# Another order for the products of layer 0 beside an eigensolver: turned rows in place, W3 in halves, G·s1 by batch

## Chip, cores and metric

One core of one Trainium2 chip. The metric is the device time of one launch in microseconds (us). Everything is float32.

## What is computed

Two residual layers with a norm ahead of each, on x (64 batches, 256 nodes, 256 features) and one adjacency matrix `adj` (256 x 256):

```python
h = relu(layernorm(x))                       # layer 0
G = adj * adj
s1 = relu(G @ (h  @ W1))                     # W1: 256 x 512
s2 = relu(G @ (s1 @ W2))                     # W2: 512 x 1024
x  = x + G @ (s2 @ W3)                       # W3: 1024 x 256
h = relu(layernorm(x))                       # layer 1
L = D^-1/2 (diag(deg) - adj) D^-1/2          # only the lower triangle counts
_, U = eigh(L)
x  = x + U @ (relu((U.T @ h) @ W1' + b1) @ W2' + b2)
```

The products of layer 0 may be bracketed in any way, and so may `(U.T @ h) @ W1'`.

## The kernel before

Two bodies of work share the core until layer 1 begins. `Eigen.vectors` finds U: 254 Householder steps (lines 252 to 331), then 32 QL steps on small blocks (lines 563 to 700), then four levels that join the blocks (lines 1024 to 1436). It is one long chain of mostly small VectorE (DVE) operations. ScalarE (ACT) takes square roots and squares in it, and TensorE (PE) turns columns into rows: the matmuls into `psA` and `psB` at line 252 come once in each Householder step. `Layers.layer0` is independent of it and consists of large products.

Layer 0 works on 32 pairs of batches. Each stage of a pair is a method of `Layers`; all products are issued by `group` (line 1527), so the trace tells them apart by tile names. A float32 matmul shows as two records.

- `begin(q)`: loads x (a tag with 2 buffers), `norm` (four ACT sums, a DVE operation, four ACT squares, then an ACT root among seven DVE operations, lines 1529 to 1551), `relu_norm` into `h0`.
- `first(q)`: y1 = turned G·h0, 16 records `bank<-gt,h` with 256 columns, four banks, copied out by ACT (line 1572).
- `second(q)`: y1·W1, 16 records `bank<-L_gnn_W,y` with 512 columns, one bank for each half m of the rows and batch b; ACT makes s1 of each bank with a relu (line 1615). Then y2 = turned G·s1, 32 records `bank<-gt,s` with 256 columns, four banks through `project`, each with both batches of one block c.
- `third(q)`: W2·y2, 64 records `bank<-y,L_gnn_W` with 512 columns, eight banks, relu into s2 (line 1625).
- `fourth(q)`: s2·W3, 64 records `bank<-L_gnn_W,s` with 256 columns, two banks (one for each half m of the rows), copied to p3 (line 1639).
- `last(q)`: G·p3, 8 records `bank<-p,gt` with 512 columns, two banks, which DVE adds to x to give x1 (line 1648); x1 goes to DRAM for all but the last two pairs; then `norm` and `relu_norm` into h1.
- `for_layer1(q)`: turns h1 by 8 transposes (`bank<-eye,h`, line 1666) in two banks, ACT copies each to `ht` (line 1669), then 16 records `bank<-L_gnn_W,ht` with 128 columns make hw (copied at line 1682, sent to DRAM).

What sets the order: each engine has one list of instructions, fixed when the program is built. A planner of the language simulates the program and gives an engine that is free the earliest instruction in the program's text that is ready. All of `eigen.vectors` is written ahead of `layer0`, so the eigensolver goes first wherever it is ready and layer 0 fills what is left, in the order of its own text. [...] The result shows in the trace: PE's list has one to ten records of layer 0 between two of the eigensolver, and in every pair the same order, `first(q+1)`, `last(q)`, `second(q+1)`, `third(q+1)`, the transposes of `for_layer1(q)`, then 2 records of hw, 2 or 4 of W3, 14 of hw, and the rest of W3.

All work tiles of layer 0 have one buffer; `ht` shares the tag and so the buffer of `p3`. Four PSUM banks (tag `bank`) go round among all stages of layer 0; the eigensolver has the other four. Layer 1 (`layer1`, lines 1754 to 1770) has its order written out by hand and begins after both; `eigen.mend`, a branch that isn't taken here, stands before it.

Of the kernel before, what the change touches and what calls it, by code (L numbers as in the profile page):

```python
# [21 lines left out]
F32 = mybir.dt.float32  # L22
# [5 lines left out]
N = 256  # L28
P = 128
H = 2  # L30
PAIRS = 32
# [1440 lines left out]
class Layers:  # L1472
# [102 lines left out]
    def layer0(self):  # L1575


        self.begin(0)
        self.first(0)
        self.second(0)  # L1580
        for q in range(PAIRS):
            if q + 1 < PAIRS:
                self.begin(q + 1)
            self.third(q)
            if q > 0:
                self.for_layer1(q - 1)
            self.fourth(q)
            if q + 1 < PAIRS:
                self.first(q + 1)
            self.last(q)  # L1590
            if q + 1 < PAIRS:
                self.second(q + 1)
        self.for_layer1(PAIRS - 1)

    def begin(self, q):
# [10 lines left out]
    def second(self, q):  # L1606

        nc, w1, y1 = self.nc, self.w["L0_gnn_W1"], self.y1.pop(q)
        s1 = self.wp.tile([P, H, 2, 512], F32, tag="s1", name="s1")
        for m in range(H):  # L1610
            for b in range(2):
                ps = self.bank()
                at = b * N + m * P
                self.group(ps, [(y1[:, c, at : at + P], w1[:, c, :]) for c in range(2)])
                nc.scalar.activation(s1[:, m, b, :], ps, AF.Relu)  # L1615
        self.y2[q] = self.project(s1, 512 // P, self.gt2, "y2")

    def third(self, q):

# [4 lines left out]
            self.group(ps, [(w2[:, c, j * P : (j + 1) * P], y2[:, c, :]) for c in range(4)])  # L1624
            nc.scalar.activation(s2[:, j, :], ps, AF.Relu)  # L1625

    def fourth(self, q):

        nc, w3, s2 = self.nc, self.w["L0_gnn_W3"], self.s2.pop(q)
        self.p3[q] = p3 = self.wp.tile([P, H, 2 * N], F32, tag="p3", name="p3")  # L1630
        for m in range(H):
            ps = self.bank()
            for b in range(2):
                at = b * N + m * P
                self.group(
                    ps[:, b * N : (b + 1) * N],
                    [(s2[:, j, at : at + P], w3[:, j, :]) for j in range(1024 // P)],
                )
            nc.scalar.copy(p3[:, m, :], ps)

    def last(self, q):

# [11 lines left out]
        self.norm(x1, scale, shift)  # L1654
        self.h1[q] = self.relu_norm(x1, scale, shift, "h1")

    def for_layer1(self, q):

        nc, h1 = self.nc, self.h1.pop(q)
        ht = self.wp.tile([P, N // P, 2 * N], F32, tag="p3", name="ht")  # L1660
        for c in range(N // P):
            ps = self.bank()
            for b in range(2):
                for h in range(H):
                    at = b * N + h * P
                    nc.tensor.transpose(  # L1666
                        ps[:, at : at + P], h1[:, h, b, c * P : (c + 1) * P], self.eye
                    )
            nc.scalar.copy(ht[:, c, :], ps)  # L1669
        hw = self.kept.tile([P, H, 2, P], F32, tag="hw", name="hw")  # L1670
        ps = self.bank()
        for h in range(H):
            for b in range(2):
                at = (h * 2 + b) * P
                self.group(
                    ps[:, at : at + P],
                    [
                        (ht[:, c, b * N + h * P : b * N + (h + 1) * P], self.w["L1_gnn_W1"][:, c, :])
                        for c in range(N // P)
                    ],  # L1680
                )
        nc.scalar.copy(hw.rearrange("p h b k -> p (h b k)"), ps)  # L1682
        if q in self.spilled:
            nc.sync.dma_start(out=self.spilled_hw[q], in_=hw.rearrange("p h b k -> p (h b k)"))
        else:
            self.hw[q] = hw
# [142 lines left out]
```

## Time and profile before

| | us |
|---|---|
| median of 3 runs | 2566.05 (2566.05 to 2566.56) |
| the profiled execution | 2568.63, of which its span is 2566.5 |
| the eigensolver's Householder steps end | about 1400 |
| its QL steps | 1437 to 1805 |
| its last DVE work | about 2250 |
| the last product of layer 0 ends | 2395.6 |
| layer 1 | 2396 to 2566 |

The profile has a row of busy time for each engine, tables of busy time by stretch of time, lists of who waited for whom, and a timeline of each engine. "PE" is matmuls, "PEld" the loads of the stationary operand. "bank<-gt,s" means: writes a tile `bank`, reads `gt` and `s`. In a timeline, "[3.22 <-ACT s L1615]" means that the engine was idle for 3.22 us just before and that ACT's instruction of line 1615, which writes tile s, ended that. Full-speed rows of a product start 0.429 us apart at 512 columns, 0.216 at 256 and 0.110 at 128 (medians over all pairs of neighbours of one kind).

### The profile page before, as it was taken

What the parts mean: (1) busy time and instruction counts of PE and PEld (TensorE: products, weight loads), DVE (VectorE), ACT (ScalarE), POOL (GpSimd) and SP (SyncE); (2) the same over time, 40 slices, a digit from 0 to 9 for tenths busy, and PEclk for the clock granted to TensorE, in tenths of its full rate; (3) what the DMA queues carried; (4) which work ended last, traced back from release to release, by engine and by line L of the source; (5) the groups of instructions that cost most, each with busy time, mean ns of one, the idle gap of its engine ahead of it and who ended that gap; (6) DMA issues with size and microseconds to landing.
All of it is one profiled execution on the core that took longest, in us unless ns stands there. A gap on an engine that the chain in (4) does not pass through costs nothing. (4 is left out here: it accounts for less than half of the span.)

```text
span 2566.5 us, 38939 instructions
## 1 busy us (share of the span) xinstructions
PE 2457.2 (96%) x8986; PEld 1524.1 (59%) x8986; DVE 2186.7 (85%) x13785; ACT 1025.5 (40%) x3080; POOL 473.7 (18%) x2006
## 2 busy tenths in 40 slices
PE   7999999999999999999999998899999999999899
PEld 4566566556665555555555555556556656666688
DVE  7999999999999999999999999999889899810343
ACT  4444344444443344444434433333444342343322
POOL 1222222222222233333332000000000000000343
PEclk9999999999999999999999999999999999999999
DMA  3000000000000000000000000000000000020376
GB/s 114 17 21 21 21 5 21 21 17 22 21 22 21 5 22 22 17 22 22 22 7 20 17 21 22 21 22 5 25 22 21 21 21 12 14 71 1 123 252 208
DMA packets 59405, 90.07 MB, mean 35 GB/s; under 512 B 5792, under 2 KB 42784, under 8 KB 59168
## 3 DMA queue, kind: packets, MB, share of 16 engines
q1 hardware_dynamic: 59168, 87.52, 10.3%
q8 instruction: 74, 1.21, 0.2%
q14 instruction: 163, 1.34, 0.2%
HBM read 47.13 MB, written 40.37 MB: 34 GB/s over the span
## 5 line engine op out<-in xcount | busy, mean ns | idle before, releaser
L1527 PE MATMUL bank<-y,L_gnn_W 128*128 128x512 f32 x2048 | 923.4, 593 | 0.0
L1527 PEld LDWEIGHTS bank<-y,L_gnn_W 128*128 128x128 f32 x2048 | 373.4, 192 | 369.6 <-issue 350.5
L1527 PE MATMUL bank<-L_gnn_W,s 128*128 128x256 f32 x2048 | 474.5, 380 | 0.0
L1527 PEld LDWEIGHTS bank<-L_gnn_W,s 128*128 128x128 f32 x2048 | 377.3, 192 | 44.6 <-ACT s L283 0.3
L1625 ACT ACTIVATE s<-bank 128x512 f32<-128x512 f32 x256 | 151.3, 592 | 297.7 <-PE bank L1527 296.9
L1527 PE MATMUL bank<-gt,s 128*128 128x256 f32 x1024 | 249.6, 392 | 18.6 <-ACT s L1615 18.3
L1527 PE MATMUL bank<-L_gnn_W,y 128*128 128x512 f32 x512 | 234.4, 594 | 4.9 <-DVE x L1648 3.2
L1527 PEld LDWEIGHTS bank<-gt,s 128*128 128x128 f32 x1024 | 195.2, 198 | 64.2 <-ACT s L1615 29.2
L1727 POOL TENSOR_TENSOR xb<-x,ub 128x512 f32<-128x512 f32 x64 | 79.8, 1269 | 650.3 <-DVE x L1648 558.1
L273 ACT ACTIVATE junk<-xr 128x254 f32<-128x254 f32 (+63 forms) x254 | 77.9, 307 | 300.8 <-DVE xr L131 298.7
L274 POOL COPY alpha<-xr 128x1 f32<-128x1 f32 x254 | 100.8, 397 | 497.0 <-DVE xr L131 478.5
L1527 PEld LDWEIGHTS bank<-L_gnn_W,y 128*128 128x128 f32 x512 | 92.7, 191 | 103.6 <-issue 80.1
L1557 ACT ACTIVATE h<-x,shift,scale 128x256 f32<-128x256 f32 x256 | 133.8, 589 | 40.0 <-DVE shift L1551 39.8
L1536 ACT ACTIVATE junk<-x 128x256 f32<-128x256 f32 x256 | 106.0, 414 | 87.9 <-DVE x L1648 73.8
L1572 ACT COPY y<-bank 128x512 f32<-128x512 f32 x192 | 109.9, 577 | 77.3 <-PE bank L1527 76.9
L131 DVE SCALAR_TENSOR_TENSOR A<-wr,uc,A 128x255 f32<-128x255 f32 (+63 forms) x381 | 139.7, 367 | 0.0
L1540 ACT ACTIVATE junk<-x,nm 128x256 f32<-128x256 f32 x256 | 129.2, 505 | 18.3 <-DVE nm L1537 12.2
L252 PEld LDWEIGHTS psA<-ident,A 128*128 128x128 f32 x381 | 51.0, 134 | 143.8 <-PE bank L1527 63.0
L327 POOL TENSOR_TENSOR e<-nb,alpha 128x1 f32<-128x1 f32 x254 | 48.2, 190 | 458.2 <-DVE nb L139 433.3
L131 DVE SCALAR_TENSOR_TENSOR q<-q 128x1 f32<-128x1 f32 (+1 forms) x576 | 121.1, 210 | 12.9
L131 DVE SCALAR_TENSOR_TENSOR A<-xr,wc,A 128x255 f32<-128x255 f32 (+63 forms) x381 | 128.7, 363 | 0.0
L252 PEld LDWEIGHTS psB<-ident,ac 128*128 128x128 f32 x381 | 44.0, 134 | 136.3 <-PE bank L1527 68.5
(623 smaller groups left out, 4611.7 us busy)
## 6 DMA issues: line engine op xcount, KB each, us to landing
x<-x SPq DMA_DIRECT2D x60, 512.0 KB, 3.6
x<-in_x_dram SPq DMA_DIRECT2D x64, 256.0 KB, 3.8
out_dram<-out SPq DMA_DIRECT2D x64, 256.0 KB, 2.2
hw<-hw SPq DMA_DIRECT2D x60, 256.0 KB, 2.7
L_gnn_W<-in_L_gnn_W_dram SPq DMA_DIRECT2D x1, 2048.0 KB, 10.9
L_gnn_W<-in_L_gnn_W_dram SPq DMA_DIRECT2D x1, 1024.0 KB, 13.4
L_gnn_W<-in_L_gnn_W_dram SPq DMA_DIRECT2D x1, 512.0 KB, 6.3
mask<-in_c_blk_dram SPq DMA_DIRECT2D x2, 256.0 KB, 2.8
```

Source lines behind the costliest of these rows:

```text
L131: return self.nc.vector.scalar_tensor_tensor(out, in0, scalar, in1, op0, op1, accum_out=accum)
L252: nc.tensor.transpose(ps[:, h * P : (h + 1) * P], column[:, h : h + 1].to_broadcast([P, P]), ident[:, 0, 0:P],)
L273: nc.scalar.activation(sq[:, rest], xr[:, rest], AF.Square, accum_out=tail)
L274: nc.gpsimd.tensor_copy(alpha, xr[:, lo : lo + 1])
L327: nc.gpsimd.tensor_tensor(e0, nb, alpha, OP.add)
L1527: self.nc.tensor.matmul(out, lhsT=lhsT, rhs=rhs, start=i == 0, stop=i == len(pairs) - 1)
L1536: nc.scalar.activation(junk, x[:, j // 2, j % 2, :], AF.Copy, accum_out=s[:, j : j + 1])
L1540: nc.scalar.activation(junk, x[:, j // 2, j % 2, :], AF.Square, bias=nm[:, j : j + 1], accum_out=v[:, j : j + 1])
L1557: self.nc.scalar.activation(h[at], x[at], AF.Relu, bias=shift[:, j : j + 1], scale=scale[:, j : j + 1])
L1572: self.nc.scalar.copy(out[:, c, :], ps)
L1625: nc.scalar.activation(s2[:, j, :], ps, AF.Relu)
L1727: nc.gpsimd.tensor_tensor(xb[:, :, b, :], x1[:, :, b, :], self.ub2, OP.add)
```

## The change

Each product keeps its records, sizes and count; so do the copies and the DVE work. What changes is the order of the program's text in a pair's turn of the loop:

| | before | after |
|---|---|---|
| 1 | begin(q+1) | begin(q+1) |
| 2 | third(q): W2 | third(q): W2 |
| 3 | transposes, copies and hw of q-1 | transposes and copies of q-1 (`turn_rows`) |
| 4 | W3, both halves | W3, half 0 |
| 5 | first(q+1) | hw of q-1 (`for_layer1`) |
| 6 | last(q) | first(q+1) |
| 7 | second(q+1) | W3, half 1 |
| 8 | | second(q+1) |
| 9 | | last(q) |

In `second`, the W1 banks of batch 0 come first, then those of batch 1; G·s1 is then done for batch 0 (two banks, each with two blocks c) and after that for batch 1. The copy to y2 writes two runs of 256 columns instead of one of 512. `turn_rows` takes two banks, transposes into both, and only then copies both back into the buffer of h1 itself, so that `ht` is no longer a tile and `p3` has its buffer alone.

```diff
         for q in range(PAIRS):
-            if q + 1 < PAIRS:
+            more = q + 1 < PAIRS
+            if more:
                 self.begin(q + 1)
             self.third(q)
             if q > 0:
+                self.turn_rows(q - 1)
+            self.fourth(q, 0)
+            if q > 0:
                 self.for_layer1(q - 1)
-            self.fourth(q)
-            if q + 1 < PAIRS:
+            if more:
                 self.first(q + 1)
+            self.fourth(q, 1)
+            if more:
+                self.second(q + 1)
             self.last(q)
-            if q + 1 < PAIRS:
-                self.second(q + 1)
+        self.turn_rows(PAIRS - 1)
         self.for_layer1(PAIRS - 1)
...
         s1 = self.wp.tile([P, H, 2, 512], F32, tag="s1", name="s1")
-        for m in range(H):
-            for b in range(2):
+        for b in range(2):
+            for m in range(H):
                 ps = self.bank()
                 at = b * N + m * P
                 self.group(ps, [(y1[:, c, at : at + P], w1[:, c, :]) for c in range(2)])
                 nc.scalar.activation(s1[:, m, b, :], ps, AF.Relu)
-        self.y2[q] = self.project(s1, 512 // P, self.gt2, "y2")
+        self.y2[q] = y2 = self.wp.tile([P, 512 // P, 2 * N], F32, tag="y2", name="y2")
+        for b in range(2):
+            for c in range(0, 512 // P, 2):
+                ps = self.bank()
+                for i in range(2):
+                    at = (c + i) * P
+                    self.group(
+                        ps[:, i * N : (i + 1) * N],
+                        [(s1[:, h, b, at : at + P], self.gt2[:, h, :]) for h in range(H)],
+                    )
+                nc.scalar.copy(
+                    y2[:, c : c + 2, b * N : (b + 1) * N], ps.rearrange("p (c n) -> p c n", c=2)
+                )
...
-    def fourth(self, q):
...
-        for m in range(H):
...
+    def fourth(self, q, m):
+
+        nc, w3, s2 = self.nc, self.w["L0_gnn_W3"], self.s2[q]
+        if q not in self.p3:
+            self.p3[q] = self.wp.tile([P, H, 2 * N], F32, tag="p3", name="p3")
+        ps = self.bank()
...
-    def for_layer1(self, q):
-
-        nc, h1 = self.nc, self.h1.pop(q)
-        ht = self.wp.tile([P, N // P, 2 * N], F32, tag="p3", name="ht")
-        for c in range(N // P):
-            ps = self.bank()
+    def turn_rows(self, q):
+
+        nc, h1 = self.nc, self.h1[q]
+        banks = [self.bank() for _ in range(N // P)]
+        for c, ps in enumerate(banks):
             for b in range(2):
                 for h in range(H):
                     at = b * N + h * P
                     nc.tensor.transpose(
                         ps[:, at : at + P], h1[:, h, b, c * P : (c + 1) * P], self.eye
                     )
-            nc.scalar.copy(ht[:, c, :], ps)
+        for c, ps in enumerate(banks):
+            nc.scalar.copy(h1[:, c].rearrange("p b f -> p (b f)"), ps)
+
+    def for_layer1(self, q):
+
+        nc, ht = self.nc, self.h1.pop(q).rearrange("p c b f -> p c (b f)")
```

More of the change, by code (lines that the diff above doesn't have):

```diff
@@ L1625, in third @@
             nc.scalar.activation(s2[:, j, :], ps, AF.Relu)
-    def fourth(self, q):
-        nc, w3, s2 = self.nc, self.w["L0_gnn_W3"], self.s2.pop(q)
-        self.p3[q] = p3 = self.wp.tile([P, H, 2 * N], F32, tag="p3", name="p3")
-        for m in range(H):
-            ps = self.bank()
[L1633 to L1639, printed above, removed]
+    def fourth(self, q, m):
[3 more added lines that the diff above has]
+        ps = self.bank()
+        for b in range(2):
+            at = b * N + m * P
+            self.group(
+                ps[:, b * N : (b + 1) * N],
+                [(s2[:, j, at : at + P], w3[:, j, :]) for j in range(1024 // P)],
+            )
+        nc.scalar.copy(self.p3[q][:, m, :], ps)
     def last(self, q):
@@ L1655, in last @@
         self.h1[q] = self.relu_norm(x1, scale, shift, "h1")
-    def for_layer1(self, q):
-        nc, h1 = self.nc, self.h1.pop(q)
-        ht = self.wp.tile([P, N // P, 2 * N], F32, tag="p3", name="ht")
-        for c in range(N // P):
-            ps = self.bank()
+    def turn_rows(self, q):
+        nc, h1 = self.nc, self.h1[q]
+        banks = [self.bank() for _ in range(N // P)]
+        for c, ps in enumerate(banks):
             for b in range(2):
```

## The prediction

> **What bounds the kernel now.** I read the page's busy row and slices first, then busy time by stretch, then who waited for whom, then timelines of PE and ACT at the waits that the change is about.
>
> ```profile
> PE 2457.2 (96%) x8986; PEld 1524.1 (59%) x8986; DVE 2186.7 (85%) x13785; ACT 1025.5 (40%) x3080; POOL 473.7 (18%) x2006
> PE   7999999999999999999999998899999999999899
> DVE  7999999999999999999999999999889899810343
> ```
>
> The first row of slices must be read against the second: PE is full from end to end, DVE is as full until the eigensolver ends at slice 35. Two full engines side by side: which one gives way decides the gain.
>
> ```profile
> 64.00:800.00 736.00, 727.61 (x2709) 432.97 (x2709) 717.63 (x4229) 321.71 (x998) 189.44 (x812) 1.00 0.06 19
> 800.00:1400.00 600.00, 582.27 (x2096) 332.26 (x2095) 576.15 (x4263) 265.01 (x917) 186.78 (x1051) 1.00 0.06 19
> 1400.00:1800.00 400.00, 370.60 (x1297) 233.38 (x1297) 370.82 (x2953) 143.51 (x405) 7.53 (x36) 0.98 0.05 17
> 1800.00:2255.00 455.00, 431.60 (x1525) 271.73 (x1524) 398.50 (x1960) 179.16 (x503) 0.48 (x2) 0.98 0.06 22
> 2255.00:2396.00 141.00, 129.52 (x451) 81.14 (x449) 11.84 (x37) 46.83 (x114) 9.87 (x8) 0.96 0.07 25
> ```
>
> The columns are the stretch, its length, and the busy time of PE, PEld, DVE, ACT and POOL. PE is idle 8, 18, 29, 23 and 11 us in these stretches; busy time flatters it, so I also took, from the starts of all PE records in the timeline, the time between neighbours over the full-speed distance (0.429, 0.216, 0.110 us). By the record that came late:
>
> | us lost before | 64-800 | 800-1400 | 1400-1800 | 1800-2255 | 2255-2396 |
> |---|---|---|---|---|---|
> | eigensolver's records | 26.6 | 40.2 | 1.8 | 11.7 | 0 |
> | hw | 3.7 | 3.7 | 13.7 | 12.4 | 3.4 |
> | G·s1 | 0.5 | 0.0 | 19.0 | 12.8 | 0.7 |
> | W1, last | 0.1 | 0.1 | 10.1 | 0.1 | 0.1 |
> | transposes | 0 | 0 | 0 | 1.6 | 11.0 |
>
> The change aims at hw, G·s1, W1 and last: 80 us, of which 2.5 (hw of the last pair) and the 11.0 of the last transposes lie behind the end of layer 0, where nothing can be put between. So 77.8 us can be reached, 68 of them between 1400 and 2255. What ends these waits:
>
> ```profile
> PE bank L1527 <- ACT ht L1669: 22.3, 27, 4.8
> PE bank L1527 <- ACT s L1615: 20.0, 15, 3.4
> ACT rts L608 <- DVE cs L139: 101.5, 25, 9.7
> DVE x L1648 <- PE bank L1527: 78.5, 6, 54.0
> ```
>
> Each row gives the sum, how many, the longest. PE waits for ACT, and the third row says why ACT is late: line 608 is the eigensolver's root in a QL step, and ACT stands before it until DVE delivers. The fourth is the opposite wait; 74 of its 78 us come after 2255 (in the timeline, 19.8 and 54.0), so while the eigensolver runs DVE practically never waits for layer 0.
>
> ```profile
> 1484.28 0.23 ACT L608 ACTIVATE rts<-cs 128x32 f32<-128x32 f32 x1 [6.11 <-DVE cs L139]
> 1485.52 0.22 ACT L630 ACTIVATE q<-q 128x15 f32<-128x15 f32 x1 [1.01 <-DVE q L131]
> 1485.64 0.57 ACT L1639 COPY p<-bank 128x512 f32<-128x512 f32 x1
> 1495.89 0.23 ACT L608 ACTIVATE rts<-cs 128x32 f32<-128x32 f32 x1 [9.69 <-DVE cs L139]
> 1496.03 0.57 ACT L1639 COPY p<-bank 128x512 f32<-128x512 f32 x1
> ```
>
> From one root to the next is 11.6 us, DVE's step, and ACT has been waiting for up to 9.7 of them. The second p copy stands behind the root though its bank was ready. Here layer 0 runs ahead and is held by its place in ACT's list. Of 31 roots' intervals, those with W2 alone carry three banks, 3 x 8 x 0.429 = 10.3 us of PE for 11.6 us of time: PE must be idle 1.3 us in each, wherever it waits.
>
> [...] the p copy just shown waits behind another instruction's wait. [...] the busy row shows 109 us of idle PE, distances between starts 202.
>
> **The change, part by part.** Records, copies, DVE operations and transfers keep their number and size, so only waits count. The moves pass no queue of POOL; the x1 store and the loads of the next x keep their order on SP and only shift with `last`.
>
> *Cover per pair.* hw gets W3's half 0 between it and the copies (32 x 0.216 = 6.9 us); last gets `second` (14 us) behind its second p3 copy in place of first (3.4); first's y1 copies get 6.9 in place of 3.4 us; G·s1 had 1.7 us for batch 0 and 0.9 for batch 1 after the last W1 bank, and gets 3.4 each. y2 now has `last` (3.4) ahead of W2. W3's half 0 loses hw ahead of it (2 us), but its first use of the last s2 block comes 3 us in; I price that at nothing. Cover exceeds nearly all waits of the rows above (longest 5.0). If time were PE's waits, 77.8 us would go.
>
> *What comes in their place.* From 800 to 2255 DVE is the limit (followed back from the eigensolver's end, the chain of work is 59 to 95% DVE in each 200 us there). PE's list is fixed, and DVE passes through it at its own pace: what PE saves at G·s1 it waits later, at the next ACT or eigensolver record. The gain is then not the wait removed but how much more of layer 0 the planner places beside a given piece of the eigensolver, since that is taken off the 140 us after 2255, where PE alone sets the pace.
>
> *How much more it places.* In the Householder steps this can be counted: the PE time of layer 0's records between two `psB` groups is what the planner thought fits. Over 248 steps it falls smoothly (6.1 us early to 3.3 late, scatter 0.26). Fitted with DVE's layer-0 operations allowed for, a step with W1 to G·s1 holds 0.06 +-0.07 us less than others, so the planner saw no wait there; a step with transposes to hw holds 0.45 +-0.07 less, the most that it saw there. The W3 records amid hw are its filling of that gap. I take 0.3 us a pair (between 0 and 0.45, as part may be its price of 128-column records): 29 pairs x 0.3 = **8.7 us** (0 to 13).
>
> *64 to 800.* PE holds 39 to 76% of the same chain here. 4.3 us of waits go; the added work takes 10 x 0.3 of it; half of the rest: **0.7 us**.
>
> *QL steps.* Intervals with W1 and norm together on ACT last 12.3 to 12.8 us with no wait of ACT before the root: ACT's crowd delays the chain. The norm of x1 moves beside W2, where ACT has little to do. Two DVE additions (2 x 0.68) explain most of the excess; I take 0.4 us for five pairs: **2.0 us** (0 to 5).
>
> *After 2255.* 0.7 at G·s1 and 0.9 at hw: **1.6 us**. The last pair's tail (9.5 us until h, then ht, then hw) stays.
>
> *The wait that grows.* h1 must be ready when W2 ends. Before, from last to the transposes was 45 to 48 us and h1 was done after 17 to 28; now W2 alone is between, 27 to 32 us. Behind the transposes stand all of PE's list, the eigensolver's records too. Usually it fits; I price it at nothing, with the upper end below.
>
> Sum 8.7 + 0.7 + 2.0 + 1.6 = 13 us against the profiled execution, 2568.6 to 2555.6. That execution is 2.6 above the median, so **2553**. About 0.2% (5.1 us) is what a measurement of this kernel tells from no change.
>
> **The rivals.**
> *All waits are real* (0.20): PE sets the time throughout, or the planner's own lists had gaps in the QL steps and levels, which PE's list there cannot show. For it: PE 96% busy. Against it: the fourth wait row, and ACT's waits at roots. At full size 2566 - 78 = 2488; likelier a part, 25 to 50 us, around 2530.
> *Nothing arrives* (0.14): the planner places the same per step, waits only move; 2563, within 0.2%.
> *Norm too late* (0.13, slower): between 1950 and 2080, in the levels, h1 was done 36.0 us (pair 25) and 47.4 us (pair 26) after last. Against 28 us of W2 this is 8 + 19 = 27 us of PE standing, with the eigensolver's matmuls queued behind. With the 13 saved: 2566 + 27 - 13 = 2580. It decides once such overruns pass 13 us together. Against it: the planner sees most of this lateness and puts W3 ahead.
>
> **How the numbers follow.** Forecast 0.53 (gains of 5 to 25 us, from the ends above). Faster 0.53 + 0.20 = 0.73, same 0.14, slower 0.13. The range 2518 to 2576 leaves out the larger half-tail of the first rival and of the last.
>
> **What would show it.** Right: the losses at hw and G·s1 fall below 10 us in all, while losses before the eigensolver's records, or at other ACT waits from 1400 to 2255, rise by most of that; the eigensolver ends within 10 us of 2255; layer 0's rest after it is some 10 us shorter. Wrong: the eigensolver ends over 20 us earlier, or PE's total loss falls by over 40 us; or transposes wait tens of us for h1.

## The result, and the profile after

| median, us | before | after |
|---|---|---|
| time | 2566.05 (2564.9 to 2567.3) | 2576.59 (2575.54 to 2577.91) |
| profiled execution, its span | 2568.63, 2566.5 | 2575.68, 2573.9 |

The changed kernel takes 1.0041 times as long (95% interval 1.0026 to 1.0056): 10.5 us **slower**, where 13 us faster had been forecast. Between the two profiled executions, which the traces show, the spans differ by 7.4 us. The other 3 us lie in the choice of executions: the one profiled of before stands 2.6 us above its median, that of after 0.9 below its own.

The busy row and slices of the changed kernel's page:

```profile
PE 2452.2 (95%) x8986; PEld 1526.4 (59%) x8986; DVE 2192.2 (85%) x13785; ACT 1034.2 (40%) x3080; POOL 473.4 (18%) x2006
PE   7999999999999999999999999899899999999799
DVE  7999999999999999999999999999889889800343
```

Nothing has left PE's row: the same 8986 records. A 7 is new in PE's third slice from the end (2381 to 2445 us), after DVE has fallen to 0. The busy time by stretch (columns: stretch, length, busy time of PE, PEld, DVE, ACT, POOL):

```profile
64.00:800.00 736.00, 725.36 (x2693) 431.06 (x2692) 714.44 (x4206) 324.71 (x994) 187.91 (x805) 1.00 0.06 19
800.00:1400.00 600.00, 580.72 (x2089) 330.92 (x2087) 576.17 (x4255) 269.35 (x918) 186.58 (x1046) 1.00 0.06 19
1400.00:1800.00 400.00, 371.34 (x1319) 237.47 (x1320) 372.10 (x2972) 144.51 (x408) 8.45 (x43) 0.98 0.05 18
1800.00:2255.00 455.00, 426.55 (x1510) 270.45 (x1509) 400.32 (x1957) 174.27 (x484) 0.46 (x2) 0.97 0.06 19
2255.00:2396.00 141.00, 126.22 (x438) 78.78 (x436) 15.77 (x41) 48.77 (x124) 9.80 (x8) 0.96 0.09 32
```

PE is idle 29 us between 1400 and 1800, as before, though the waits at which the change aimed are nearly gone. The list of waits shows what PE waits for now:

```profile
ACT rts L608 <- DVE cs L139: 131.1, 32, 8.7
...
DVE x L1665 <- PE bank L1527: 105.5, 5, 48.8
...
PE bank L1682 <- ACT h L1557: 17.9, 3, 15.2
...
PE bank L1527 <- ACT s L1642: 14.0, 7, 4.5
...
PE bank L1527 <- ACT s L1620: 12.3, 4, 4.8
...
PE bank L1527 <- ACT h L1686: 0.5, 1, 0.5
```

The last row is what the 22.3 us wait for `ht` has become (h in place, line 1686): 0.5 us. That part of the change does what it says. In its place stand 14.0 us ahead of W3 (for the last s2, line 1642), where the list of before has none, and 15.2 us in one piece ahead of transposes. By the measure of the prediction, time between PE's starts over the full-speed distance:

| us lost before | before | after |
|---|---|---|
| eigensolver's records | 93.9 | 124.1 |
| hw | 36.8 | 3.5 |
| G·s1 | 32.9 | 19.3 |
| W1, last, W2, first | 15.7 | 12.9 |
| W3 | 1.8 | 19.4 |
| transposes | 12.4 | 20.9 |

| us lost in | 64-800 | 800-1400 | 1400-1800 | 1800-2255 |
|---|---|---|---|---|
| before | 34.7 | 48.0 | 44.8 | 42.0 |
| after | 37.5 | 48.8 | 42.0 | 45.9 |

The kinds change places, and the sums of the stretches stay within 4 us. The rest of PE's idle time is moved, not removed. ACT's roots show why, in the changed kernel as before (ACT's timeline):

```profile
1486.67 0.23 ACT L608 ACTIVATE rts<-cs 128x32 f32<-128x32 f32 x1 [8.28 <-DVE cs L139]
1487.91 0.22 ACT L630 ACTIVATE q<-q 128x15 f32<-128x15 f32 x1 [1.01 <-DVE q L131]
1488.03 0.57 ACT L1656 COPY p<-bank 128x512 f32<-128x512 f32 x1
```

ACT stands 8.28 us before the root, and a p copy goes after it at once. DVE still deals out the time. The waits that are left at G·s1 from 1400 on are of this kind: at 1511.9, 1581.2, 1652.9 and 1804.9 us (5.0, 1.3, 4.4, 2.2 us) the s1 copy that PE needs stands behind a root that waits for DVE, for 5.4 to 8.5 us, so that 3.4 us of cover don't reach.

**Where the 7.4 us are.** From one mark in the trace to the next, in us: the first Householder step, the Householder steps, the passage to QL, the QL steps, the levels, then layer 0 from the eigensolver's last DVE work to the last product of `last(31)`, then the tail from there to layer 1, then layer 1.

| | start | Householder | to QL | QL | levels | layer 0 after | tail | layer 1 | span |
|---|---|---|---|---|---|---|---|---|---|
| before | 28.9 | 1372.4 | 35.8 | 367.5 | 443.8 | 131.1 | 16.8 | 170.2 | 2566.5 |
| after | 27.3 | 1376.6 | 35.3 | 365.0 | 447.4 | 129.1 | 23.0 | 170.2 | 2573.9 |
| difference | -1.6 | +4.2 | -0.5 | -2.5 | +3.6 | -2.0 | **+6.2** | 0 | +7.4 |

The eigensolver is 4.8 us longer from the Householder steps to its end; layer 0's rest after it is 2.0 us shorter, not 10; and the tail of the last pair grows by 6.2 us. The Householder steps lose their 4.2 us before 800: step 120 comes 771.3 us after the first, in before 766.7. The 3.6 us of the levels are the least certain figure of the row, because before's own levels scatter: in the kernel before without its branch (below), whose lists are the same up to the end of the levels, they took 439.3 us at a granted clock of 0.988 (the share of PE's full clock that the profile shows as granted), here 443.8 at 0.977. Four kernels with the order of after took 447.0 to 447.4. So the levels lose 3 to 8 us, and the missing 3 us of the median may lie there.

The tail first, in the timeline of before:

```profile
2380.13 0.69 DVE L1648 TENSOR_TENSOR x<-x,bank 128x512 f32<-128x512 f32 x1 [1.03 <-PE bank L1527]
2380.90 7.37 POOL L1727 TENSOR_TENSOR xb<-x,ub 128x512 f32<-128x512 f32 x6 [59.81 <-DVE x L1648]
...
2389.59 0.69 PE L1666 MATMUL bank<-eye,h 128*128 128x128 f32 x2 [9.49 <-ACT h L1557]
```

The second addition of the last pair follows its product, and 9.5 us later the rows are turned. The timeline of after:

```profile
2379.54 0.69 DVE L1665 TENSOR_TENSOR x<-x,bank 128x512 f32<-128x512 f32 x1 [39.18 <-PE bank L1527]
...
2383.81 0.69 DVE L1712 TENSOR_REDUCE u<-u 128x2 f32<-128x512 f32 x1 [3.58 <-ACTq L1468]
...
2384.41 0.68 DVE L1665 TENSOR_TENSOR x<-x,bank 128x512 f32<-128x512 f32 x1
...
2385.93 9.80 POOL L1748 TENSOR_TENSOR xb<-x,ub 128x512 f32<-128x512 f32 x8 [567.54 <-ACT junk L1536]
...
2393.34 1.19 DVE L1549 TENSOR_SCALAR s<-s 128x4 f32<-128x4 f32 x1
...
2396.43 0.69 PE L1682 MATMUL bank<-eye,h 128*128 128x128 f32 x2 [15.21 <-ACT h L1557]
```

The additions are 4.87 us apart instead of 1.72, though both products ended by 2381.2. Between them stands a wait on line 1468: that is the **branch of `mend`**, which isn't taken, but is in the list of every engine (a load of a flag, a compare, a jump over the repair). In before it stood elsewhere: on PE between the transposes and hw of pair 30. `mend` is the last of the text, so the planner puts it where PE has nothing else ready once the eigensolver is done. That was the gap before hw, which the change closes; the next is after the last product. On DVE the branch falls between the two additions (from the end of its compare at 2380.24 to 2383.15), on ACT amid the four sums of the norm (2381.38 to 2383.76). What comes behind it in the text goes with it: the `turn` work of line 1712, and GpSimd's xb operations, which now run until 2395.7. While they do, the norm's small DVE operations, but for the reciprocals (0.18), take 0.73 to 1.19 us: line 1549 takes 1.19 here, and 0.17 in before. So the tail's 6.2 us are 3.15 between the additions and 2.56 from the second addition to the transposes (12.02 against 9.46), which is what the operations of lines 1537, 1549 and 1551 take longer (0.75 + 1.02 + 0.80); 0.5 is left over.

So there were three questions: whether the branch's place costs those 6 us; what the cover is worth where PE and not DVE sets the time; and which part of the new order keeps the planner from placing more of layer 0.

### The profile page after: what moved, and what is told of

It reads as the page before. It is cut to its first block, busy times and chain, and to the rows that moved or that the text cites. A ratio compares the mean times of both kernels' runs of the same rounds, so it can differ in the third digit from the quotient of the medians.

```text
span 2573.9 us, 38943 instructions
## 1 busy us (share of the span) xinstructions
PE 2452.2 (95%) x8986; PEld 1526.4 (59%) x8986; DVE 2192.2 (85%) x13785; ACT 1034.2 (40%) x3080; POOL 473.4 (18%) x2006
## 5 line engine op out<-in xcount | busy, mean ns | idle before, releaser
L1527 PE MATMUL bank<-gt,s 128*128 128x256 f32 x1024 | 242.8, 387 | 12.3 <-ACT s L1620 12.3
L1665 DVE TENSOR_TENSOR x<-x,bank 128x512 f32<-128x512 f32 x64 | 43.5, 681 | 105.5 <-PE bank L1527 105.5
## 6 DMA issues: line engine op xcount, KB each, us to landing
L_gnn_W<-in_L_gnn_W_dram SPq DMA_DIRECT2D x1, 2048.0 KB, 10.5
L_gnn_W<-in_L_gnn_W_dram SPq DMA_DIRECT2D x1, 1024.0 KB, 13.3
```

Source lines behind the costliest of these rows:

```text
L1527: self.nc.tensor.matmul(out, lhsT=lhsT, rhs=rhs, start=i == 0, stop=i == len(pairs) - 1)
L1665: nc.vector.tensor_tensor(flat(x1)[:, m, :], flat(x)[:, m, :], ps, OP.add)
```

## Experiments

Medians in us; each is beside runs of the kernel before on the same chip, whose median stands in brackets.

### The branch

**Only the last pair in the old order** (hw of pair 30 directly behind its copies, so that the branch finds its old gap), against after:

```diff
+            if q > 0 and not more:
+                self.for_layer1(q - 1)
             self.fourth(q, 0)
-            if q > 0:
+            if q > 0 and more:
                 self.for_layer1(q - 1)
```

> The changed kernel, but in the last pair's turn of the loop hw of pair 30 follows its transposes directly, as before the change; in the built lists the branch of mend is then found between those transposes and hw again, not after the last products. Theory tail (the branch and the work behind it fell into the last pair's norm): the wait of PE before the last transposes falls from 16.7 us to about 11, the time by 5 to 6 us, to about 2571. Rival order (the new order costs time in all pairs, and the tail is by the way): at most 1 us back, 2575 to 2577.

Measured: 2577.1 (2566.03), 1.0045 [1.0031, 1.0059]. A miss as a time, and instructive. The tail did fall, from 23.0 to 17.6; but "layer 0 after" rose from 129.1 to 134.3, and layer 1 took 171.9 us for 170.2. The timeline of this kernel:

```profile
2362.10 0.59 ACT L1688 COPY h<-bank 128x512 f32<-128x512 f32 x1 [0.22 <-PE bank L1684]
...
2365.52 0.59 ACT L1688 COPY h<-bank 128x512 f32<-128x512 f32 x1 [2.83 <-ACTq L1468]
...
2366.16 3.36 PE L1527 MATMUL bank<-L_gnn_W,h 128*128 128x128 f32 x14 [2.49 <-ACT h L1688]
```

The branch is in the old gap, between ACT's two copies. ACT spends 2.83 us there, and PE waits. In before the same passage cost ACT 0.42 us:

```profile
2293.89 0.58 ACT L1669 COPY ht<-bank 128x512 f32<-128x512 f32 x1
...
2294.89 0.59 ACT L1669 COPY ht<-bank 128x512 f32<-128x512 f32 x1 [0.42 <-ACTq L1468]
```

So the branch has no fixed price; what the long passages have in common stands in the last section. Layer 1 has the same order of work in all kernels; it took 170.0 to 170.2 us in the seven traces in which its granted clock was 0.997 or more, and 171.8 to 172.0 in the four in which it was 0.986 or 0.987, of which this is one. This run doesn't put a price on the place of the branch; the next does.

**The branch called ahead of the last pair**, all else as after:

```diff
         for q in range(PAIRS):
             more = q + 1 < PAIRS
+            if not more:
+                branch()
...
-        layers.layer0()
-        eigen.mend(u, ut)
+        layers.layer0(lambda: eigen.mend(u, ut))
```

> The changed kernel, order of all products kept; only the branch of mend is called in the program's text ahead of the last pair's turn of the loop instead of after layer 0, so that it is met before W2 of pair 31. Theory tail: as in the run beside it, 5 to 6 us less than the changed kernel, about 2571, with the eigensolver's end still 3 us later than before the change. Rival order: no change beyond 1 us.

Measured: 2572.37 (2566.03), 1.0026 [1.0017, 1.0036]: **4.2 us** less than after, a little under the 5 to 6 expected. Its span is 3.5 us shorter: the tail is 5.4 shorter, while layer 1 is 1.8 longer, again at the lower clock (0.986). The tail is 17.6 us, and in its timeline the addition, the short operation of line 1549 and the wait of 9.49 us are back:

```profile
2381.33 0.69 DVE L1667 TENSOR_TENSOR x<-x,bank 128x512 f32<-128x512 f32 x1 [1.03 <-PE bank L1527]
...
2389.51 0.17 DVE L1549 TENSOR_SCALAR s<-s 128x4 f32<-128x4 f32 x1
...
2390.78 0.69 PE L1684 MATMUL bank<-eye,h 128*128 128x128 f32 x2 [9.49 <-ACT h L1557]
```

**Both kernels without the branch** (neither can then repair a failed eigensolver; its last operations, the test that sets the flag, stay in the text):

```diff
         layers.layer0()
-        eigen.mend(u, ut)
```

> The kernel before with mend left out (a repair of the eigenvectors that is not taken with these data; it is the only thing left out). Both theories: 2563 to 2567, since the branch stood in a gap of PE that was there anyway. It is the base for the next one.

> The changed kernel with mend left out likewise. Theory tail: the distance to the kernel before without mend shrinks from 10.5 us to 2 to 4 us. Rival order: it stays at 7 to 11 us.

Measured: 2566.52 (1.0004 [0.9996, 1.0013]) and 2571.41 (1.0025 [1.0015, 1.0036]), with before at 2566.03. Before loses nothing that can be measured by its branch, after 5.2 us. Without it the two are still 4.9 us apart, between the two forecasts, so the branch explains half of the result, and not the absence of the gain. By the marks of these two traces the rest lies in the eigensolver: the Householder steps take 3.7 us longer (1376.4 for 1372.7) and the levels 7.7 (447.0 for 439.3), QL 2.5 less; the tails are equal (19.6 and 19.3). Both tails are longer than 17.6, and in both GpSimd's xb runs beside the whole norm: lines 1549 and 1551 take 1.8 us longer together.

### The parts alone

Each on the kernel before.

```diff
-        for m in range(H):
-            for b in range(2):
+        for b in range(2):
+            for m in range(H):
...
-        self.y2[q] = self.project(s1, 512 // P, self.gt2, "y2")
+        self.y2[q] = y2 = self.wp.tile([P, 512 // P, 2 * N], F32, tag="y2", name="y2")
+        for b in range(2):
+            for c in range(0, 512 // P, 2):
+                ps = self.bank()
...
```

> The kernel before with one part of the change: W1 banks and G s1 by batch. Theory pace (DVE sets the time, PE's savings come back as waits elsewhere): PE's loss before G s1 falls from 33 us to under 15, its loss before the eigensolver's records or elsewhere rises as much, time within 2 us of 2566. Rival cover (waits of PE are time): 2566 less about 15.

```diff
-            self.last(q)
             if q + 1 < PAIRS:
                 self.second(q + 1)
+            self.last(q)
```

> The kernel before with one part of the change: last after second, so that y2 and p3 are covered and the norm of x1 begins 14 us later, next to the norm of the following x. Theory norm (the Householder steps take 4 us longer because DVE now meets steps of the two norms in its list for which ACT isn't ready): Householder steps 1376 to 1377 us against 1372.4, the idle time of DVE in them up by 2 to 3. Rival: 1372 to 1373, so that another part of the change lengthens them.

```diff
             if q > 0:
+                self.turn_rows(q - 1)
+            if q > 0 and not more:
                 self.for_layer1(q - 1)
-            self.fourth(q)
-            if q + 1 < PAIRS:
+            self.fourth(q, 0)
+            if q > 0 and more:
+                self.for_layer1(q - 1)
+            if more:
                 self.first(q + 1)
+            self.fourth(q, 1)
             self.last(q)
...
```

> The kernel before with one part of the change: rows turned in place, W3 in halves with hw between transposes' copies and its use, first between the halves; last follows W3's second half and second follows last as before; the last pair keeps transposes and hw together. Theory pace: PE's loss before hw falls from 37 us to about 10, time within 3 us of 2566; Householder steps 1372 to 1373. Rival cover: 2566 less about 25.

| alone | median (2566.83) | ratio | loss at its target | where it came back |
|---|---|---|---|---|
| G·s1 by batch | 2572.28 | 1.0023 [1.0013, 1.0033] | G·s1 32.9 to 5.8 | W2 2.9 to 14.7, W1 6.5 to 14.6, eigensolver's 93.9 to 108.5 |
| last behind `second` | 2586.64 | 1.0077 [1.0063, 1.0090] | W1, last 10.6 to 8.7 | eigensolver's 93.9 to 112.6, first 2.2 to 11.5 |
| W3 in halves, rows turned in place | 2565.7 | 0.9996 [0.9988, 1.0005] | hw 36.8 to 4.2 | last 4.1 to 23.5, W1 to 14.2, eigensolver's to 113.7 |

Two of three are slower alone, one is equal. For G·s1 by batch neither forecast came true: it was to lie within 2 us or to save 15, and costs 5.5. The Householder steps of W3 in halves take 1374.8 us, not 1372 to 1373. The waits of W3 in halves, against those of `ht` and s in before:

```profile
PE bank L1527 <- ACT p L1646: 16.5, 5, 6.1
...
PE bank L1527 <- ACT s L1622: 8.5, 11, 2.2
```

Again the wait has gone to the next product that needs an ACT copy, here `last`, behind the p copies. The sums by stretch stay within 4.5 us of before's in the three, but for one: from 1400 to 1800 it is 44.8 in before and 43.9 with last behind `second`, from 1800 to 2255 some 42 in before and 52 there.

Then I counted what the theory named as the only gain: how much of layer 0 stands in PE's list ahead of a given product of the eigensolver (records times their full-speed distance, in us; it is a count of the list, no time). Differences from before:

| more placed ahead of | end of Householder | end of QL | last product | layer 0 after, us |
|---|---|---|---|---|
| G·s1 by batch alone | -4.3 | -6.0 | -9.0 | +7.8 |
| last behind `second` alone | -2.6 | -6.0 | -12.9 | +13.3 |
| W3 in halves alone | **+4.3** | +4.3 | **+6.9** | -7.2 |
| after | 0.0 | -0.9 | -0.9 | -2.0 |

The last column, measured in time, follows the count: what isn't placed ahead is left for later. The whole time need not follow. W3 in halves leaves 7.2 us less after the eigensolver, but its median is only 1.1 below before's, since the eigensolver itself takes longer. Alone, only the cover at hw buys place and the other two parts lose it. The parts don't add (-9.0 - 12.9 + 6.9 = -15.0, in the change -0.9), so these two prices hold for each part alone.

That `last` behind `second` lengthens the Householder steps (1379.4 against 1372.4) was more than expected. The rows of what DVE waits for from 64 to 1400, before, after, and last behind `second` alone:

```profile
DVE rs L142 <- ACT s L283: 0.6, 2, 0.3
...
DVE nm L1537 <- ACT junk L1536: 0.2, 1, 0.2
```

```profile
DVE rs L142 <- ACT s L283: 1.6, 4, 1.1
DVE nm L1537 <- ACT junk L1536: 1.4, 7, 0.2
...
DVE v L1543 <- ACT junk L1540: 0.3, 1, 0.3
```

```profile
DVE rs L142 <- ACT s L283: 2.3, 5, 1.1
DVE nm L1537 <- ACT junk L1536: 1.1, 6, 0.2
...
DVE v L1543 <- ACT junk L1540: 0.3, 1, 0.3
```

DVE waits for ACT where before it hardly did: for the eigensolver's root (line 283) and for the sums of the norm. DVE's idle time in these steps is 43.1 us in before, 46.4 in after and 47.8 with last alone: 3.3 and 4.7 more, of which these rows name 2.5 and 2.9. The norm of x1 now stands beside the norm of the next x, since `last` comes directly before `begin`. The last experiment below puts `last` ahead of W1 again, and DVE's idle time is back at 43.2; so it goes with the place of `last`, though the two norms alone were not moved. The rest of the longer steps (DVE's own work there, each operation until its end or the next one's start, 1278.6 against 1279.7 and 1280.8) is spread over many operations, and is open, as are the longer levels.

### Layer 0 without the eigensolver

The same edit on both kernels: `vectors` and `mend` are left out, u and ut are copies of the adjacency matrix, so that DVE (9% busy on both pages) and ACT (37 and 38%) are mostly free for layer 0, and PE (98 and 99%) sets the time.

```diff
-        eigen.vectors(u, ut)
+        eigen.laplacian()
+        tc.nc.vector.tensor_copy(u, eigen.adj)
+        tc.nc.vector.tensor_copy(ut, eigen.adj)
         layers.layer0()
-        eigen.mend(u, ut)
```

> The kernel before with the eigensolver left out (only its laplacian, which also makes G, stays; U is a copy of adj, so that layer 1 computes with another matrix; the branch is out too). PE alone sets the time. Theory pace: PE's loss per pair is 1 to 3 us in this order, all at G s1, hw, last, so that the time is about 2200 to 2320.

> The changed kernel with the same left out. Theory pace (the cover works, but only where PE sets the time): 30 to 80 us less than the one beside it, losses at G s1, hw and last near nothing. Rival (the new order does not save PE's waits even there): within 10 us of it.

Measured: 2302.2 (2301.5 to 2303.18) for the old order, 2273.61 (2271.86 to 2273.95) for the new: **28.6 us less**, just under the 30 to 80 forecast. PE's waits, old order:

```profile
PE bank L1527 <- ACT ht L1669: 9.2, 32, 0.3
...
PE bank L1527 <- ACT s L1615: 6.3, 31, 0.6
```

New order:

```profile
PE bank L1682 <- ACT h L1557: 7.2, 2, 7.0
...
PE bank L1527 <- ACT h L1686: 0.5, 1, 0.5
```

Each of 31 pairs waited 0.3 us for ht and 0.2 for s1; by distances between starts it was 17.8 us at hw and 14.0 at G·s1, some 1 us a pair, and both are gone but for the last pair. So the order covers what it was meant to cover. Beside the eigensolver this cover brought no time.

### The position of last

**All of the change but `last` behind `second`**, the branch ahead of the last pair: `last` stands after both halves of W3 and `first`, ahead of W1; G·s1 is then behind W1, by batch. Against after:

```diff
-            if more:
-                self.first(q + 1)
             self.fourth(q, 1)
             if more:
+                self.first(q + 1)
+            self.last(q)
+            if more:
                 self.second(q + 1)
-            self.last(q)
...
```

> The changed kernel with last(q) moved back to stand between first(q+1) and second(q+1), W3's second half ahead of first, and the branch of mend called ahead of the last pair's turn. In the built list of PE 1949.1 us of layer 0's records stand ahead of the eigensolver's last product; the kernel before has 1941.8, the changed one 1940.9. Theory placed (what counts is how much of layer 0 the planner sets beside the eigensolver, less what DVE loses there): 8 us less left over, the Householder steps 2 us longer as with W3 by halves alone, no tail: 2560 to 2564. Rival (the placed amount is no guide): 2567 to 2573 as with the branch moved alone.

> The same order without moving the branch; in the built list of PE it stands after the last products of layer 0, as in the changed kernel. Theory tail: 4 to 6 us more than the run beside it. Rival: the place of the branch costs under 1.5 us.

Measured: 2566.51 (2566.91), 0.9999 [0.9990, 1.0007]; and with the branch late 2571.3, 1.0017 [1.0011, 1.0024], 4.8 us more, tail 17.6 to 23.0, as expected and the second time that the branch costs this. Of the first, the size was missed. It places 7.3 us more than before (4.3 by the end of Householder), and layer 0 after the eigensolver is 9.1 us shorter, which is the size forecast for the change. But Householder is 3.8 us longer, the levels 1.9, layer 1 1.8 (172.0 for 170.2): 7.5 of 9.1 are given back. Layer 1's part goes with its granted clock (0.986 for 0.997). In the Householder steps it is not idle time of DVE (43.2 against 43.1 us) but DVE's own work (1282.2 against 1278.6); why that takes longer is open. The spans differ by 1.1 us, the medians by less. G·s1 by batch, which alone costs 9.0 us of place, costs none in this company: 7.3 with it, 6.9 in W3 in halves without it. No version beat the kernel before by more than can be measured.

## Why the prediction was wrong

The 10.5 us divide so. The branch: 4.2, from 2576.59 to 2572.37. With the branch ahead of the last pair in both, `last` behind `second` against ahead of W1 (with W3's second half and G·s1 on the other side of it) is 1.0026 against 0.9999 of before, about 6.9 us. That leaves nothing for the rest of the change; by the intervals above each of the two figures is uncertain by 3 to 4 us.

- **Waits move where DVE sets the pace: right.** The sums by stretch from 64 to 2255 changed by -2.8 to +3.9 us, while hw alone lost 33. Had PE's waits been real, 2488 to 2530 would have come. The new waits are before the eigensolver's records (+30.2), W3 (+17.6) and, in the tail, transposes.
- **"How much more it places", 8.7 us: the step that failed.** The term itself was nearly right where it was made alone: W3 in halves places 4.3 us more over some 18 pairs of the Householder steps, 0.24 a pair (forecast 0.3), and 6.9 in all. But I asked only what the closed gap adds, and treated the moves of G·s1 and of `last` as cover without a price. In the planner's list they have one: alone -9.0 and -12.9; in the whole, the placed work is 0.9 less than before. With `last` ahead of W1 it is 7.3 more, so 8.2 us are lost by the order around `last`. The step before it, that more placed work is taken off the time, failed too: with 6.9 and 7.3 us more placed, near the 8.7 of the forecast, the medians fell by 1.1 and 0.4 us, within what can be measured, since the eigensolver's Householder steps took 2.4 and 3.8 us longer beside it and its levels 1.1 and 1.9. The prediction had no term for an eigensolver that gets longer. The fit that found no wait at W1 to G·s1 said what there was to gain there, not what moving the work would lose.
- **64 to 800, 0.7 us gained: wrong in sign.** The Householder steps are 4.2 us longer, all of it before 800. Part is DVE waiting for ACT, shown above; I had counted PE's waits here and not DVE's for ACT, which in before were 0.6 and 0.2 us.
- **QL, 2.0 us: right in size**, 2.5 measured, but not shown to be for the reason given. That was the norm of x1 beside W2; `last` behind `second` alone, which moves it, shortens QL by 1.5 us, and G·s1 by batch alone, which leaves it where it was, by 2.9.
- **The levels** had no term; they are 3.6 us longer in these two executions, and 7.7 between the two kernels without the branch.
- **After 2255, 1.6 us: too small against what it met**; layer 0's rest is 2.0 shorter in all, where 8.7 + 1.6 was forecast.
- **"The last pair's tail stays": failed, 6.2 us.** I asked whether an instruction of the tail changes, and not what floats in the lists. The branch was free in a gap; the change closed that gap, and the branch went to the next one, which was on the critical path. On DVE the second addition stood behind the branch and the sum of line 1712 for 3.2 us with its product ready (ended by 2381.2, added at 2384.41).
- **W3's half 0 without hw ahead of it, priced at nothing:** PE waits 14.0 us there. They are among the waits that moved, and no run prices them as time.
- **Transposes waiting for h1, priced at nothing: right on PE.** Apart from the last pair they wait 4.3 us in all, not the rival's 27. The norm's new place costs elsewhere, in DVE's waits and in the count of placed work. The rival had the right sign and the wrong place; that its 2580 lies near the 2577 measured is luck, since its 27 us of transposes were 4.3.

Of the signs named in advance: the loss at hw fell to 3.5 us, that at G·s1 only to 19.3, so the two are not below 10 together; the losses before the eigensolver's records and at other ACT waits rose by about what fell; the eigensolver's end came within 10 us (3.2 later); layer 0's rest was to be some 10 us shorter and was 2.0.

Term by term against the profiled execution: 8.3 us of gain missing in layer 0's rest, 4.9 in Householder, 3.6 in the levels, 6.2 in the tail, less 0.5 more gain in QL and 2.1 at the start and before QL: 20.4, from -13 to +7.4.

## What to carry to other kernels

Where one engine sets the pace and another's list is fixed, as with DVE and PE here, covering the second one's waits may only move them (33 us less was lost at hw, and the sums by stretch changed by -2.8 to +3.9): count how much of its work stands ahead of the pace-setter's marks, and price every move in that count, also the moves that only make room. Then ask whether the pace-setter gets longer beside more work: here 7 us more were placed and almost none of them gained. When a gap is closed, look for what the planner had put into it, here the branch, and find out where that lands next. Before a change, run the stage without its rival for the engines: 28.6 us there and none in the whole say at once which of the two sets the time.

## What was not expected of the hardware

- The same branch over `mend`'s repair was passed at very different cost; only its place in the lists differed. From the start of its compare to the first instruction behind the jump, ACT took 0.45 us in five traces, 0.84 in one, and 2.43, 2.49 and 2.73 in three; DVE took 2.88 to 3.09 in all nine traces that hold the branch, GpSimd 0.46. Packets of the DMA queues that the page lists as `instruction` (q8 and q14, 74 and 163 packets in after) tell the cases apart. Within ACT's passage in after (2381.33 to 2383.76) the trace has two of them, within that in before (2294.36 to 2294.81) none. In ACT's three slow passages a packet of 8 KB starts 0.92 or 0.93 us after the compare, in all nine of DVE 1.04 to 1.08 us after it. None starts within ACT's five quick passages, or within GpSimd's. So ACT's three slow passages and DVE's nine go with such a packet. That the engine waits for it fits these times and was not tried by itself; why a packet comes in one passage of ACT and not in another is open.
- Tiny DVE operations of the norm (128x4 elements) take long beside GpSimd's xb operations (128x512, 1.27 us each). Over all traces the scalings and two-input operations took 0.10 to 0.18 us without an xb operation beside them, and 0.19 to 1.19 us with one (57 cases); the 26 two-input operations among these never took under 0.72. In before, line 1548 took 1.18 us at 2387.10, and line 1549 0.17 us at 2388.32, just after GpSimd's last xb ended at 2388.27; in after, where xb runs to 2395.7, line 1549 took 1.19. It took 1.19 in all four kernels in which xb lasted that long, and 0.17 in the seven with the eigensolver in which it didn't. None of these operations is longer than one xb operation (1.19 against 1.27 us). The scalings of lines 1537, 1543 and 1549 have one input and are slowed too (0.95, 1.09 and 1.19 us in after), while the reciprocals, with one input as well, stay at 0.18. What slows them is shown by no run here.
